# A graph-attention layer on one core: the node stage in two passes, normalization on ScalarE and VectorE, ten early sections gathered raw, and edge targets held in whole sections

## The chip, the cores and the metric

The kernel runs on one core of a Trainium2 chip. The metric is the device time of one execution in microseconds. A core has TensorE (PE, matmuls), VectorE (DVE), ScalarE (ACT), GpSimd (POOL, which here also issues the indirect DMAs that gather rows) and SyncE (SP, which issues most other DMAs).

## The reference

There are N = 12500 nodes with C = 128 channels and E = 400000 edges, sorted by their target node `dst`. Cut to what matters:

```python
h       = relu(layernorm(x))                       # N x 128
msg_src = h @ w_src + b_src                        # N x 128
msg_dst = h @ w_dst                                # N x 128
message = msg_src[src] + msg_dst[dst]              # E x 128
message = message * edge_weight * radial_mlp(edge_attr)
message = message @ w_sep + b_sep                  # E x 256: alpha and value, 8 heads
score   = einsum(smooth_leaky_relu(alpha), alpha_dot)
att     = softmax of score over the edges of one target node
out     = segment_sum(value * att, dst) @ w_proj + b_proj
return x + out
```

## The kernel before, in words

The program has two stages. The **node stage** holds x as 98 tiles of 128 nodes, four to a quad, 25 quads. For a quad, `stats` takes sums by VectorE, `scales` the root (ScalarE) and the reciprocal and shift (VectorE), `norm` the normalized rows (two of four tiles on ScalarE, two on POOL), `turn` four TensorE transposes and one VectorE copy with the relu, and `products(i, k)` the matmuls by w_src (k = 0) or w_dst (k = 1), a ScalarE copy out of PSUM into `ms`, and the store to the tables `t_src` and `t_dst` in HBM, issued by SP. A loop over the quads interleaves these; the w_dst products follow ten quads behind the w_src products.

Between them stand other preparations. `load_targets` brings `dst` on chip as 128 partitions x 3125 targets, and the first and last target of each section and the first of the next by strided DMAs of single words. `falls` compares neighbours for order, `fits` sums the violations into `bad`, `marks` writes a flag for every edge whose target differs from the next (times the constant RESTART) to `same`, `spans`, `cuts` and `direct_ids` prepare windows of target nodes. Everything after the node stage stands behind `if bad == 0`, for which each engine loads `bad` and branches.

The **edge stage** goes over 391 steps k of two sections (f = 0, 1), a section being 512 edges in 4 tiles of 128. For every tile POOL issues one indirect DMA that gathers 128 rows of t_src (line 1018, 8 a step). Steps below 13 (`AHEAD`) have places of their own in `early`, which lie where the messages do (shown as mT in the trace); from step 13 on, the tiles gs0 and gs1 are used with `GSB` = 5 buffers each, so gather k + 5 writes where gather k was read. The first steps, `RAW` = 4 of them, gather rows of x instead of t_src during the node stage (`raw_gather`, 8 a step, line 354). These are normalized and turned (`raw_scales`, `raw_norm`, `raw_turn`) there, and multiplied by w_src in the edge stage (line 1074), where other steps have TensorE transposes of the gathered rows (line 1078). Then line 1095 forms the message `mT` on VectorE, line 1101 multiplies by the alpha weights, and 12 steps later (`LAG`) lines 1233 and 1246 form values and segment sums. `prep_load`, `prep_make` and `prep_turn` bring the source indices of 16 steps, as the gathers need them.

The order of the code is the order on each engine; nothing reorders it. The semaphores say who waits for whom.

Of the kernel before, what the change touches and what calls it, by code (L numbers as in the profile page):

```python
# [44 lines left out]
RAW = 4  # L45
# [10 lines left out]
def gnn_kernel(ctx: ExitStack, tc: tile.TileContext, a: dict, out: bass.AP):  # L56
# [45 lines left out]
    groups = [(t, min(t + XG, NF)) for t in range(0, NF, XG)]  # L102
# [8 lines left out]
    def blocks(t0, t1):  # L111
# [19 lines left out]
    part8 = const.tile([P, 1], F32, name="part8")  # L131
    nc.vector.tensor_scalar(part8, part, float(H), None, op0=ALU.mult)
    spread = const.tile([MQ, P], BF16, name="spread")
    below = const.tile([MQ, P], F32, name="below")
    nc.vector.tensor_scalar(below, lane[:MQ, :], part8[:MQ], None, op0=ALU.subtract)
    above = const.tile([MQ, P], F32, name="above")
    nc.vector.tensor_scalar(above, below, 0.0, None, op0=ALU.is_ge)
    nc.vector.scalar_tensor_tensor(spread, below, float(H), above, op0=ALU.is_lt, op1=ALU.mult)
    spread4 = const.tile([MQ, P], BF16, name="spread4")
    nc.vector.tensor_copy(spread4.rearrange("i (j b h) -> i j b h", j=4, b=4),  # L140
                          spread.rearrange("i (b j h) -> i j b h", b=4, j=4))
# [39 lines left out]
    with tc.tile_pool(name="node", bufs=2) as np_, tc.tile_pool(name="node1", bufs=1) as n1, \  # L181
# [23 lines left out]
        cur = n1.tile([P, CC + 1], I32, name="cur")  # L205
        nc.vector.memset(cur[0:1, 0:1], -1)
        NH = NS // 17
        ends = n1.tile([NH, 17, 2], I32, name="ends")
# [7 lines left out]
        def load_targets():  # L216

            nc.sync.dma_start(out=cur[:, 1:CC + 1], in_=dst.rearrange("(p c) -> p c", p=P))
            at = dst[CC - 1:CC]
            with nc.allow_non_contiguous_dma(reason="single targets"):  # L220
                nc.sync.dma_start(out=cur[1:P, 0:1], in_=bass.AP(at.tensor, at.offset, [[CC, P - 1], [1, 1]]))
                at = dst[0:1]
                h = NH - 1
                nc.sync.dma_start(out=ends[0:h], in_=bass.AP(
                    at.tensor, at.offset, [[34 * SEC // 2, h], [SEC, 17], [SEC - 1, 2]]))
                at = dst[h * 17 * SEC:h * 17 * SEC + 1]
                nc.sync.dma_start(out=ends[h:NH, 0:16, :], in_=bass.AP(
                    at.tensor, at.offset, [[1, 1], [SEC, 16], [SEC - 1, 2]]))
                at = dst[(NS - 1) * SEC:(NS - 1) * SEC + 1]
                nc.sync.dma_start(out=ends[h:NH, 16, :], in_=bass.AP(  # L230
                    at.tensor, at.offset, [[1, 1], [E - 1 - (NS - 1) * SEC, 2]]))
                at = dst[SEC:SEC + 1]
                nc.sync.dma_start(out=nexts[0:h], in_=bass.AP(at.tensor, at.offset, [[17 * SEC, h], [SEC, 17]]))
                at = dst[(h * 17 + 1) * SEC:(h * 17 + 1) * SEC + 1]
                nc.sync.dma_start(out=nexts[h:NH, 0:16], in_=bass.AP(at.tensor, at.offset, [[1, 1], [SEC, 16]]))

        nexts = n1.tile([NH, 17], I32, name="nexts")
        nc.vector.memset(nexts, 0)
# [50 lines left out]

        def scales(t0, t1):  # L290
            s = slice(t0, t1)
            nc.scalar.activation(rstd[:, s], mv[:, s, 2], AF.Sqrt, bias=eps, scale=1.0 / C)
            nc.vector.reciprocal(rstd[:, s], rstd[:, s])
            nc.vector.scalar_tensor_tensor(shift[:, s], mv[:, s, 1], -1.0, rstd[:, s],
                                           op0=ALU.mult, op1=ALU.mult)

        def norm(i):
            t0, t1 = quads[i]
            hs[i] = np_.tile([P, 4, C], F32, name="h", bufs=4)
            for t in range(t0, t1):  # L300
                n = rows(t)
                if t - t0 < 4 - 2:
                    nc.scalar.activation(hs[i][:n, t - t0, :], x_all[:n, t, :], AF.Identity,
                                         bias=shift[:n, t:t + 1], scale=rstd[:n, t:t + 1])
                else:
                    nc.gpsimd.tensor_scalar(hs[i][:n, t - t0, :], x_all[:n, t, :], rstd[:n, t:t + 1],
                                            shift[:n, t:t + 1], op0=ALU.mult, op1=ALU.add)
# [50 lines left out]
        def raw_scales(q0, q1):  # L358
# [6 lines left out]
            nc.scalar.activation(rstdr[:, s], mvr[:, s, 2], AF.Sqrt, bias=eps, scale=1.0 / C)  # L365
            nc.vector.reciprocal(rstdr[:, s], rstdr[:, s])
            nc.vector.scalar_tensor_tensor(shiftr[:, s], mvr[:, s, 1], -1.0, rstdr[:, s],
                                           op0=ALU.mult, op1=ALU.mult)

        def raw_norm(q):  # L370
            v = raw(q).rearrange("p (t c) -> p t c", c=C)
            hs["raw", q] = h = np_.tile([P, 4, C], F32, name="h", bufs=4)
            for t in range(4):
                u = slice(4 * q + t, 4 * q + t + 1)
                if t < 2:
                    nc.scalar.activation(h[:, t, :], v[:, t, :], AF.Identity, bias=shiftr[:, u], scale=rstdr[:, u])
                else:
                    nc.vector.tensor_scalar(h[:, t, :], v[:, t, :], rstdr[:, u], shiftr[:, u],
                                            op0=ALU.mult, op1=ALU.add)
# [17 lines left out]

        gt = n1.tile([P, CC], BF16, name="gt")

# [5 lines left out]
        def fits():  # L405
            cnt = n1.tile([P, 1], F32, name="cnt")
            nc.vector.memset(cnt, 0.0)
            span = n1.tile([NH, 2, 17], F32, name="span")
# [4 lines left out]
            nc.vector.tensor_reduce(cnt[:NH, :], span.rearrange("p a b -> p (a b)"), AX.X, ALU.add)  # L413
            tot = nps.tile([1, BANK], F32, name="tot", bufs=1)
            for o in range(0, CC, BANK):
                w = min(BANK, CC - o)
                nc.tensor.matmul(tot[:, :w], ones_b, gt[:, o:o + w], start=(o == 0), stop=False,
                                 skip_group_check=True)
# [16 lines left out]
            nc.sync.dma_start(out=ends_d[:, 1:2 * NS + 1].rearrange("o (p c) -> (o p) c", p=NH),  # L435
                              in_=ends.rearrange("p s i -> p (s i)"))
# [94 lines left out]
        sm = n1.tile([P, CC], BF16, name="sm")  # L531
        past = n1.tile([1, NX + 1 - E], BF16, name="past")

        def marks(j):
            s_ = slice(j * CC // 4, (j + 1) * CC // 4)
            nc.vector.tensor_tensor(sm[:, s_], cur[:, s_], cur[:, s_.start + 1:s_.stop + 1], op=ALU.not_equal)
            nc.vector.tensor_scalar(sm[:, s_], sm[:, s_], RESTART, None, op0=ALU.mult)
            if j == 3:
                nc.sync.dma_start(out=same[:, 0:E].rearrange("o (p c) -> (o p) c", p=P), in_=sm)
                nc.sync.dma_start(out=same[:, E:NX + 1], in_=past)  # L540

        for i in range(3):
            stats(*quads[i])
            scales(*quads[i])
            norm(i)
            if i == 0:
                turn(0)
                nc.gpsimd.memset(past, RESTART)
                first()
        for i in (3, 4):  # L550
            stats(*quads[i])
        scales(quads[3][0], quads[4][1])
        more = iter(weights_list())
        for i in range(Q):
# [10 lines left out]
            if i % 2 and i + 4 < Q:  # L565
                scales(quads[i + 4][0], quads[min(i + 5, Q - 1)][1])
# [19 lines left out]
            if i == 22:  # L586
                direct_ids()
        for t in range(Q, 4 * RQ):
            raw_gather(t)
        for i in range(Q - 10, Q):  # L590
            q = i - (Q - 10)
            products(i, 1)
            if 0 <= q - 1 < RQ:
                raw_turn(q - 1)
            if q in (1, 4):
                raw_scales(4 + q // 2, 6 + q // 2)
            if q < RQ:
                raw_norm(q)
        nc.scalar.activation(silu, eps[0:1, :], AF.Silu)

# [312 lines left out]
    def windows():  # L913
# [7 lines left out]
        with tc.tile_pool(name="ps", bufs=1, space=PSUM) as pp, \  # L921
# [568 lines left out]
            def step(k):  # L1490
# [20 lines left out]
                if k % 16 == 8 and has(k + 8):  # L1511
# [337 lines left out]
```

## Time and profile before

| what | us |
|---|---|
| runs before (median of 3) | 4083.88 (4075.56 to 4085.45) |
| profiled execution, its own time | 4089.07 |
| its span | 4087.2 |
| mean granted TensorE clock | 0.985 |
| TensorE busy | 3865.2 (95%) |
| VectorE busy | 3104.5 (76%) |
| POOL busy | 3065.6 (75%) |
| ScalarE busy | 1862.3 (46%) |

In rows of the profile a line number (L1018) is one of the kernel before; "out<-in" names what is written and read, "xN" counts instructions; a timeline row begins with the start and the duration in us and ends with the idle time before it and what released it. A group row has the busy sum, the mean of one in ns, and the idle time before its instructions. In a table of windows the columns are the window, its length, and the busy time (with count) of PE, PEld, DVE and POOL for the named tile, the granted clock, the share of DMA time and GB/s.

### The profile page before, as it was taken

The numbers are of one execution on the slowest core, as the hardware profiler recorded it, in microseconds if no ns is written. First come the engines' busy times: TensorE is split into PE (matmuls) and PEld (weight loads), VectorE is DVE, ScalarE is ACT, GpSimd is POOL, SyncE is SP. The second block draws the span as 40 slices with busy tenths as digits, with TensorE's granted clock in tenths as the row PEclk, the third lists the DMA queues.
The fourth block names the chain that finished last, engine by engine and source line by source line (L and its number), as shares of the span: only waits on it lengthen the run. The fifth ranks groups of instructions, "written<-read, shape, count | busy, mean of one in ns | idle before, by whom it ended". The sixth has DMA issues, their size and how long they took to land.

```text
span 4087.2 us, 84249 instructions
## 1 busy us (share of the span) xinstructions
PE 3865.2 (95%) x27811; PEld 2349.3 (57%) x27811; DVE 3104.5 (76%) x5557; ACT 1862.3 (46%) x3782; POOL 3065.6 (75%) x3244
## 2 busy tenths in 40 slices
PE   7899999999999999999999999999999999999997
PEld 6356555655555555555555555555555556556555
DVE  6677777777777777777777777777777777777777
ACT  5454444444444444444444444444444444444451
POOL 6777777777777777777777777777777777777775
PEclk9999999999999999999999999999999999999998
DMA  7777777677767777777777777777777777777772
GB/s 242 214 186 194 182 193 193 184 182 190 191 169 195 186 191 172 196 187 180 185 192 185 190 189 197 194 174 192 197 194 183 185 191 198 182 195 193 186 177 55
DMA packets 536579, 762.21 MB, mean 186 GB/s; under 512 B 126743, under 2 KB 339769, under 8 KB 536006
## 3 DMA queue, kind: packets, MB, share of 16 engines
q1 hardware_dynamic: 378142, 498.27, 41.8%
q0 software_dynamic: 101872, 207.34, 24.5%
q10 hardware_dynamic: 56120, 51.10, 4.5%
q8 instruction: 226, 3.70, 0.4%
q14 instruction: 219, 1.79, 0.2%
HBM read 632.27 MB, written 125.70 MB: 185 GB/s over the span
## 4 chain that ended last, share of the span: by engine, by line
PE 68%; DMA 12%; POOL 7%; issue 5%; DVE 5%; ACT 2%; SPq 1%; ACTq 0%; DVEq 0%; POOLq 0%
PE V L1233 15%; PE pa L1101 14%; DMA gs<-t_src,idx 8%; PE misc L1246 8%; PE pm L1078 7%; PE p L1062 6%; POOL gs L1018 6%; PE m L1034 5%; PE pm L1090 4%; PE p L1047 4%; PE m L1118 3%; DMA agg<-ob 1%; DVE mT L1095 1%; POOL mT L1018 1%; DMA win<-ob 1%
## 5 line engine op out<-in xcount | busy, mean ns | idle before, releaser
L1018 POOL DMA_INDIRECT gs<-t_src,idx x3021 | 2875.4, 952 | 923.0 <-issue 768.5
L1103 ACT ACTIVATE sl<-pa,c_b_a 128x512 f32<-128x512 f32 x782 | 537.6, 687 | 1089.2 <-PE pa L1101 1085.1
L1108 DVE SCALAR_TENSOR_TENSOR al<-pa,sl 128x512 f32<-128x512 f32 x782 | 536.8, 686 | 527.6 <-ACT sl L1103 520.5
L1233 PEld LDWEIGHTS V<-c_w_v,mT 128*128 128x128 f32 x6154 | 753.3, 193 | 309.9 <-DVE ob L1250 119.9
L1233 PE MATMUL V<-c_w_v,mT 128*128 128x128 f32 x6154 | 886.3, 287 | 8.1 <-DVE pvx L1235 8.1
L1101 PE MATMUL pa<-mT,c_w_a 128*128 128x512 f32 x1564 | 839.2, 619 | 26.6 <-DVE mT L1095 23.5
L1235 DVE TENSOR_TENSOR pvx<-V,Pem 128x512 f32<-128x512 f32 x770 | 528.4, 686 | 207.9 <-PE V L1233 191.1
L1049 ACT ACTIVATE h<-p,b 128x512 f32<-128x512 f32 x391 | 469.2, 1200 | 427.5 <-PE p L1047 328.4
L1078 PEld LDWEIGHTS pm<-ident,gs 128*128 128x128 f32 x3021 | 375.2, 141 | 481.9 <-issue 463.8
L1067 DVE SCALAR_TENSOR_TENSOR rad<-p,c_fc_b,w_b 128x1024 f32<-128x1024 f32 x391 | 500.5, 1280 | 105.6 <-PE p L1062 87.3
L1246 PEld LDWEIGHTS misc<-pvx,oh 128*64 128x64 f32 x6250 | 353.1, 138 | 295.0 <-ACT h L1037 284.5
L1078 PE MATMUL pm<-ident,gs 128*128 128x128 f32 x3021 | 458.6, 275 | 64.5 <-DMA gs<-t_src,idx 64.4
L1095 DVE SCALAR_TENSOR_TENSOR mT<-pm,c_b_src,rad 128x1024 f32<-128x1024 f32 x391 | 497.6, 1273 | 7.7 <-PE pm L1090 7.2
L1246 PE MATMUL misc<-pvx,oh 128*64 128x136 f32 x6250 | 453.2, 287 | 0.9 <-ACT h L1037 0.3
L1062 PE MATMUL p<-h,w3b 64*128 64x512 f32 x1564 | 405.9, 596 | 0.5 <-ACT h L1049 0.4
L1034 PE MATMUL m<-eT,w1b 64*128 64x256 f32 x782 | 276.7, 434 | 20.3 <-ACT qT L1328 15.1
L1090 PE MATMUL pm<-ohT,m 64*128 64x512 f32 x1564 | 287.3, 445 | 0.0
L1101 PEld LDWEIGHTS pa<-mT,c_w_a 128*128 128x128 f32 x1564 | 237.3, 192 | 76.8 <-DVE mT L1095 44.5
L1034 PE MATMUL misc<-eT,w1b 64*128 64x256 f32 x782 | 276.8, 434 | 0.0
L1037 ACT ACTIVATE h<-misc,b 128x256 f32<-128x256 f32 x391 | 185.4, 474 | 193.9 <-PE misc L1034 181.1
L1134 ACT ACTIVATE Sp<-m,b_s 128x512 f32<-128x512 f32 x192 | 131.8, 686 | 308.5 <-PE m L1118 302.0
L1217 DVE TENSOR_TENSOR oh<-lane,misc 128x504 f32<-128x504 f32 x391 | 261.2, 668 | 0.1
(216 smaller groups left out, 3550.8 us busy)
## 6 DMA issues: line engine op xcount, KB each, us to landing
w_b<-in_edge_weight SPq DMA_DIRECT2D x390, 512.0 KB
d_b<-in_dst SPq DMA_DIRECT2D x390, 256.0 KB
e_t<-in_edge_attr ACTq DMA_DIRECT2D x386, 128.0 KB
sc_d<-Sp SPq DMA_DIRECT2D x192, 256.0 KB
gs<-t_src,idx POOLq DMA_INDIRECT x3021
win<-ob SPq DMA_DIRECT2D x390, 68.0 KB
agg<-ob SPq DMA_DIRECT2D x762, 33.5 KB
md<-t_dst SPq DMA_DIRECT2D x782, 32.0 KB
```

The source lines that it names most:

```text
L1018: sent = [nc.gpsimd.indirect_dma_start(out=gs[:, t, :], out_offset=None, in_=t_src[:, :], in_offset=bass.IndirectOffsetOnAxis(ap=idx[:, t0 ...
L1034: nc.tensor.matmul(p1[f], w1b[s, :], eTs[k][s, :], start=True, stop=True)
L1062: nc.tensor.matmul(p3[:, f, 0:SEC], w3b[s, :], h2s[k][s, :], start=True, stop=True)
L1067: nc.vector.scalar_tensor_tensor(rad[:, 0:n], p3.rearrange("c f e -> c (f e)")[:, 0:n], b3, w_g[k][:, 0:n], op0=ALU.add, op1=ALU.mult)
L1078: turned = [nc.tensor.matmul(pm[:, t * T:(t + 1) * T], gs[:, t, :], ident, start=(t == 0), stop=False, is_transpose=True, skip_group_check ...
L1095: nc.vector.scalar_tensor_tensor(mTs[k][:, 0:n], pms.rearrange("c f e -> c (f e)")[:, 0:n], b_n, rad[:, 0:n], op0=ALU.add, op1=ALU.mult)
L1101: nc.tensor.matmul(pa[:, 0:n], w_a, mTs[k][:, f * SEC:f * SEC + n], start=True, stop=True)
L1103: nc.scalar.activation(sl[:, 0:n], pa[:, 0:n], AF.Silu, bias=b_a, scale=1.0)
L1108: nc.vector.scalar_tensor_tensor(al, pa, 0.25, sl, op0=ALU.mult, op1=ALU.add)
L1233: nc.tensor.matmul(V[:, t, :], mTs[c][:, o:o + T], w_v, start=True, stop=True)
L1235: nc.vector.tensor_mul(pvx[c][:, f, 0:n, 0:C].rearrange("p t (h k) -> p t h k", h=H), V[:, 0:n, :].rearrange("p t (h k) -> p t h k", h=H), ...
L1246: nc.tensor.matmul(acc[f * W:(f + 1) * W, :], ohs[c][:, f * TS + t, :], pvx[c][:, f, t, :], start=(t == 0), stop=(t == n - 1), skip_group_ ...
```

## The change

The node stage is written as two passes over the quads: the first has all w_src products, the second all w_dst products and, between them, the raw rows' work, the marks and the preparations. The roots are split from the other scales. The normalized rows come from ScalarE (three of four tiles, in every third quad four) and VectorE; POOL has only two tiles of each of the first two quads. `RAW` is 5, so ten sections are gathered as rows of x, all 40 gathers issued at once after the first indices. The targets lie as 112 partitions of 7 whole sections (3584), with the word before and after; first and last targets are copied from them by VectorE (`sections`). `marks` has one operation, without RESTART, which the matrix `spread` now carries. The index preparations of the first steps are issued earlier, and the table load of the silu stands inside the second pass. The first load of x has 4 tiles of each partition.

```diff
-RAW = 4
+RAW = 5
...
-    groups = [(t, min(t + XG, NF)) for t in range(0, NF, XG)]
+    groups = [(max(t, 0), min(t + XG, NF)) for t in range(4 - XG, NF, XG)]
...
-        CC = E // P
+        SPP = -(-NS // P)
+        CC, CP = SPP * SEC, -(-NS // SPP)
+        CL = E - (CP - 1) * CC
+        SL = -(-CL // SEC)
+        assert 96 <= CP - 1 < P and 0 < CL < CC
...
-            nc.sync.dma_start(out=cur[:, 1:CC + 1], in_=dst.rearrange("(p c) -> p c", p=P))
-            at = dst[CC - 1:CC]
+            h = CP - 1
+            nc.sync.dma_start(out=cur[0:h, 1:CC + 1], in_=dst[0:h * CC].rearrange("(p c) -> p c", c=CC))
+            nc.sync.dma_start(out=cur[h:CP, 1:CL + 1], in_=dst[h * CC:E].rearrange("(p c) -> p c", p=1))
             with nc.allow_non_contiguous_dma(reason="single targets"):
-                nc.sync.dma_start(out=cur[1:P, 0:1], in_=bass.AP(at.tensor, at.offset, [[CC, P - 1], [1, 1]]))
-                at = dst[0:1]
-                h = NH - 1
-                nc.sync.dma_start(out=ends[0:h], in_=bass.AP(
-                    at.tensor, at.offset, [[34 * SEC // 2, h], [SEC, 17], [SEC - 1, 2]]))
...
+        def sections():
+
+            for e in range(2):
+                nc.vector.tensor_copy(ends[:, :, e], cur[:, 1 + e * (SEC - 1):1 + e * (SEC - 1) + (SPP - 1) * SEC + 1:SEC])
...
+        def roots(t0, t1):
+            s = slice(t0, t1)
+            nc.scalar.activation(rstd[:, s], mv[:, s, 2], AF.Sqrt, bias=eps, scale=1.0 / C)
+
         def scales(t0, t1):
             s = slice(t0, t1)
-            nc.scalar.activation(rstd[:, s], mv[:, s, 2], AF.Sqrt, bias=eps, scale=1.0 / C)
...
-                if t - t0 < 4 - 2:
+                if t - t0 < (2 if i < 2 else 4 if i % 3 == 0 else 3):
...
-                    nc.gpsimd.tensor_scalar(hs[i][:n, t - t0, :], x_all[:n, t, :], rstd[:n, t:t + 1],
+                    (nc.gpsimd if i < 2 else nc.vector).tensor_scalar(hs[i][:n, t - t0, :], x_all[:n, t, :], rstd[:n, t:t + 1],
...
-                if t < 2:
+                if t < 3:
...
             nc.vector.tensor_tensor(sm[:, s_], cur[:, s_], cur[:, s_.start + 1:s_.stop + 1], op=ALU.not_equal)
-            nc.vector.tensor_scalar(sm[:, s_], sm[:, s_], RESTART, None, op0=ALU.mult)
...
+        nc.vector.memset(past, 1.0)
+        for i in range(2):
             stats(*quads[i])
+            roots(*quads[i])
             scales(*quads[i])
             norm(i)
-            if i == 0:
-                turn(0)
-                nc.gpsimd.memset(past, RESTART)
-                first()
-        for i in (3, 4):
+        turn(0)
+        first()
+        for t in range(4 * RQ):
+            raw_gather(t)
+        for i in range(2, 5):
             stats(*quads[i])
-        scales(quads[3][0], quads[4][1])
+            if i == 2:
+                roots(*quads[i])
+                scales(*quads[i])
+                norm(i)
+        ready = quads[3][0], quads[4][1]
+        roots(*ready)
         more = iter(weights_list())
         for i in range(Q):
             if i + 1 < Q:
                 turn(i + 1)
+            if ready:
+                scales(*ready)
+                ready = None
             if i + 3 < Q:
                 norm(i + 3)
-            raw_gather(i)
-            if i >= 10:
-                products(i - 10, 1)
             products(i, 0)
             if i + 5 < Q:
                 stats(*quads[i + 5])
             if i % 2 and i + 4 < Q:
-                scales(quads[i + 4][0], quads[min(i + 5, Q - 1)][1])
+                ready = quads[i + 4][0], quads[min(i + 5, Q - 1)][1]
+                roots(*ready)
...
-            if 8 <= i < 12:
-                falls(i - 8)
-            if i == 13:
+            if i == 9:
+                sections()
+            if 10 <= i < 14:
+                falls(i - 10)
+            if i == 15:
                 fits()
-            if 14 <= i < 18:
-                marks(i - 14)
-            if i >= 9 and i % 4 == 1:
-                raw_scales(i // 4 - 2, i // 4 - 1)
-            if i == 19:
-                spans()
-            if i == 21:
-                cuts()
-            if i == 22:
-                direct_ids()
-        for t in range(Q, 4 * RQ):
-            raw_gather(t)
-        for i in range(Q - 10, Q):
-            q = i - (Q - 10)
+        extra = {2: lambda: marks(0), 4: lambda: marks(1), 6: lambda: marks(2), 8: lambda: marks(3),
+                 10: spans, 13: cuts, 15: direct_ids, 17: spreads}
+        assert 2 * RQ + 1 < Q
+        for i in range(Q):
+            if i % 2 and 0 <= i // 2 - 1 < RQ:
+                raw_turn(i // 2 - 1)
             products(i, 1)
-            if 0 <= q - 1 < RQ:
-                raw_turn(q - 1)
-            if q in (1, 4):
-                raw_scales(4 + q // 2, 6 + q // 2)
-            if q < RQ:
-                raw_norm(q)
-        nc.scalar.activation(silu, eps[0:1, :], AF.Silu)
-
+            if i % 4 == 0 and i // 2 < RQ:
+                raw_roots(i // 2, i // 2 + 2)
+            if i % 4 == 1 and i // 2 < RQ:
+                raw_scales(i // 2, i // 2 + 2)
+            if i % 2 and i // 2 < RQ:
+                raw_norm(i // 2)
+            if i in extra:
+                extra[i]()
+            if i == 2 * RQ - 2:
+                nc.scalar.activation(silu, eps[0:1, :], AF.Silu)
...
-                if k % 16 == 4 and has(k + 12):
+                if k % 16 == 4 and has(k + 12) and k > 4:
                     prep_load((k + 12) // 16)
-                if k == 2:
-                    prep_load(0)
+                if k in (-1, 0):
+                    prep_load(k + 1)
...
-                    prep_turn((k + 8) // 16)
-                if k == 4:
-                    prep_make(0)
-                if k % 16 == 7 and has(k + 9):
+                if k == 5 or k % 16 == 8 and has(k + 8) and k > 8:
+                    prep_turn((k + 11) // 16)
+                if k in (2, 4):
+                    prep_make(k // 2 - 1)
```

The order of instructions on POOL in the node stage, around the first raw gather, before (the names: h are normalized rows, mT the places of raw rows and early gathers, idx the source indices):

```order
19 L306 TENSOR_SCALAR h<-x_all,rstd,shift 128x128 [waits DMAHW4_49,DVE_49]
20 L306 TENSOR_SCALAR h<-x_all,rstd,shift 128x128
21 L354 DMA mT<-in_x,idx_172 128x128
22 L306 TENSOR_SCALAR h<-x_all,rstd,shift 128x128 [waits PE_49,Activation_49]
23 L306 TENSOR_SCALAR h<-x_all,rstd,shift 128x128
24 L354 DMA mT<-in_x,idx_172 128x128
25 L306 TENSOR_SCALAR h<-x_all,rstd,shift 128x128 [waits DVE_49,PE_49,Activation_49]
```

and of the change:

```order
12 L299 TENSOR_SCALAR h<-x_all,rstd,shift 128x128 [waits DMAHW1_49,DVE_49]
13 L299 TENSOR_SCALAR h<-x_all,rstd,shift 128x128
14 L299 TENSOR_SCALAR h<-x_all,rstd,shift 128x128 [waits DMAHW4_49,DVE_49]
15 L299 TENSOR_SCALAR h<-x_all,rstd,shift 128x128
16 L347 DMA mT<-in_x,idx_164 128x128 [waits DVE_49]
17 L347 DMA mT<-in_x,idx_164 128x128 x7
```

The pairs of normalizations between the raw gathers (they go on in the same way up to row 80) are gone, and the gathers stand together, ahead of the load of `bad`.

On TensorE, in the middle of the node stage before (pt are transposes, pm products):

```order
114 L315 MATMUL pt<-ident,h 128x128 [waits PE_49,Activation_49]
115 L315 MATMUL pt<-ident,h 128x128 [waits Activation_49]
116 L315 MATMUL pt<-ident,h 128x128 [waits Pool_49] x2
117 L326 MATMUL pm<-w_dst,x_all 128x128 [waits Activation_49]
118 L326 MATMUL pm<-w_dst,x_all 128x128 x3
119 L326 MATMUL pm<-w_src,x_all 128x128 [waits DVE_49,Activation_49]
120 L326 MATMUL pm<-w_src,x_all 128x128 x3
```

and of the change, at the border between the passes:

```order
138 L319 MATMUL pm<-w_src,x_all 128x128 [waits DVE_49]
139 L319 MATMUL pm<-w_src,x_all 84x128 [waits DMAHW3_49]
140 L319 MATMUL pm<-w_dst,x_all 128x128 [waits Activation_49]
141 L319 MATMUL pm<-w_dst,x_all 128x128 x3
142 L319 MATMUL pm<-w_dst,x_all 128x128 [waits Activation_49]
143 L319 MATMUL pm<-w_dst,x_all 128x128 x3
144 L319 MATMUL pm<-w_dst,x_all 128x128 [waits Activation_49]
145 L319 MATMUL pm<-w_dst,x_all 128x128 x3
146 L381 MATMUL pt<-ident,h 128x128 [waits Activation_49] x3
147 L381 MATMUL pt<-ident,h 128x128 [waits DVE_49]
```

The w_dst products no longer stand between the w_src products; they follow all of them, with the raw rows' transposes (line 381) among them.

More of the change, by code (lines that the diff above doesn't have):

```diff
@@ L201, in gnn_kernel @@
         b12 = const.tile([P, 2], F32, name="b12")
[L202 removed]
+        SPP = -(-NS // P)
[3 more added lines that the diff above has]
+        assert 96 <= CP - 1 < P and 0 < CL < CC
         ones_b = n1.tile([P, 1], BF16, name="ones_b")
         nc.vector.memset(ones_b, 1.0)
[L205 removed]
+        cur = n1.tile([CP, CC + 2], I32, name="cur")
         nc.vector.memset(cur[0:1, 0:1], -1)
[L207 to L208 removed]
+        nc.vector.memset(cur[96:CP, CL + 1:CC + 2], 0)
+        ends = n1.tile([CP, SPP, 2], I32, name="ends")
         eb = n1.tile([P, NS, 2], I32, name="eb")
@@ L396, in first @@
             nc.vector.tensor_copy(idx0, pt)
-        gt = n1.tile([P, CC], BF16, name="gt")
+        gt = n1.tile([CP, CC], BF16, name="gt")
         def falls(j):
@@ L407, in fits @@
             nc.vector.memset(cnt, 0.0)
-            span = n1.tile([NH, 2, 17], F32, name="span")
+            span = n1.tile([CP, 2, SPP], F32, name="span")
+            nexts = cur[:, 1 + SEC:2 + CC:SEC]
             nc.vector.tensor_sub(span[:, 0, :], ends[:, :, 1], ends[:, :, 0])
@@ L412, in fits @@
             nc.vector.tensor_scalar(span[:, 1, :], span[:, 1, :], float(W), None, op0=ALU.is_ge)
-            nc.vector.tensor_reduce(cnt[:NH, :], span.rearrange("p a b -> p (a b)"), AX.X, ALU.add)
+            nc.vector.tensor_reduce(cnt[:CP, :], span.rearrange("p a b -> p (a b)"), AX.X, ALU.add)
             tot = nps.tile([1, BANK], F32, name="tot", bufs=1)
[L415 to L418, printed above, removed]
+            assert CL >= BANK
+            for n, o0, o1 in ((CP, 0, CL), (CP - 1, CL, CC)):
+                for o in range(o0, o1, BANK):
+                    w = min(BANK, o1 - o)
+                    nc.tensor.matmul(tot[:, :w], ones_b[:n], gt[:n, o:o + w], start=(o == 0), stop=False,
+                                     skip_group_check=True)
             nc.tensor.matmul(tot[:, 0:1], cnt, ones[:, 0:1], start=False, stop=True, skip_group_check=True)
```

56 lines of the change are left out of this document (28 added, 28 removed).

## The prediction

> **What bounds the kernel now.** I read the page first, for the chain that ended last and the costliest groups.
>
> ```profile
> span 4087.2 us, 84249 instructions
> ...
> PE 3865.2 (95%) x27811; PEld 2349.3 (57%) x27811; DVE 3104.5 (76%) x5557; ACT 1862.3 (46%) x3782; POOL 3065.6 (75%) x3244
> ...
> PE 68%; DMA 12%; POOL 7%; issue 5%; DVE 5%; ACT 2%; SPq 1%; ACTq 0%; DVEq 0%; POOLq 0%
> ...
> L1018 POOL DMA_INDIRECT gs<-t_src,idx x3021 | 2875.4, 952 | 923.0 <-issue 768.5
> ```
>
> TensorE looks like the bound, 95% busy. But matmuls that are held count as busy here, and POOL's 75% hides that its gathers never pause: each is 0.95 us busy and the idle time ahead of them is almost all "issue", time in which POOL waits for nothing. So I asked for the same tile in equal windows far apart.
>
> ```profile
> 500.00:1000.00 500.00, 61.84 (x408) 50.76 (x408) 0.00 (x0) 377.76 (x398) 1.00 0.72 185
> 3000.00:3500.00 500.00, 59.13 (x392) 48.56 (x393) 0.00 (x0) 378.81 (x398) 0.99 0.74 192
> ```
>
> The last count of four is POOL's: 398 gathers in 500 us in both, 1.256 us each, 8 a step, 10.05 us a step. Then the two ends of this queue, from the timeline, with the last two stores of t_src.
>
> ```profile
> 89.92 0.32 SPq L340 DMA_DIRECT2D t_src<-ms  x1
> 90.33 0.39 SPq L342 DMA_DIRECT2D t_src<-ms  x1
> ...
> 93.89 0.94 POOL L1018 DMA_INDIRECT mT<-t_src,idx  x1 [2.97 <-DMA t_src<-ms]
> ...
> 3981.30 0.94 POOL L1018 DMA_INDIRECT gs<-t_src,idx  x1 [0.30 <-PE m L1334]
> ```
>
> Between them stand 3093 gathers (3125 tiles of 128 edges less the 32 raw ones): 3981.30 - 93.89 = 3887.4, over 3092 intervals 1.257 us each, the same as in any window, so the queue has no hole. So the time is: when the first table gather starts (it waits for the last store of t_src), plus the gathers, plus a tail of about 105 us. The change touches the first two.
>
> What limits how early the queue may run is its buffers: gather k+5 writes where the transposes of step k read. The tightest place is the first reuse, step 13 second section, against gather 18; beside it stands step 17 against gather 22.
>
> ```profile
> 227.76 0.60 PE L1078 MATMUL pm<-ident,gs 128*128 128x128 f32 x4
> 239.07 0.94 POOL L1018 DMA_INDIRECT gs<-t_src,idx  x1 [0.30 <-issue]
> ...
> 264.86 0.60 PE L1078 MATMUL pm<-ident,gs 128*128 128x128 f32 x4
> ...
> 279.06 0.95 POOL L1018 DMA_INDIRECT gs<-t_src,idx  x1 [0.30 <-issue]
> ```
>
> Read at 228.36, overwritten from 239.07: 10.7 us to spare; four steps later 265.46 and 279.06, 13.6. So the queue can move earlier by 10.7 us against TensorE's first 13 steps, not by more; after that TensorE, faster than 10.05 us a step here, gives way by itself.
>
> **The change, part by part.** The node stage's prices come from the groups of its first 112 us (busy sum, mean of one).
>
> ```profile
> L354 POOL DMA_INDIRECT mT<-in_x,idx x32 | 32.0, 1001 | 6.7 <-issue 6.0 <-PE pt L315 0.3 <-DVE ids_d L516 0.3
> L326 PE MATMUL pm<-w_src,x_all 128*128 128x128 f32 x196 | 31.0, 308 | 7.9 <-DVE x_all L317 7.4 <-ACT h L303 0.4
> L326 PE MATMUL pm<-w_dst,x_all 128*128 128x128 f32 x196 | 29.7, 302 | 0.0
> L332 ACT COPY ms<-pm 128x512 f32<-128x512 f32 (+2 forms) x52 | 27.9, 554 | 20.9 <-PE pm L326 18.7 <-issue 1.9
> L303 ACT ACTIVATE h<-x_all,shift,rstd 128x128 f32<-128x128 f32 (+1 forms) x50 | 21.9, 486 | 5.9 <-DVE shift L294 5.9
> L315 PE MATMUL pt<-ident,h 128*128 128x128 f32 x98 | 20.5, 315 | 13.6 <-POOL h L306 9.5 <-ACT h L303 3.4
> L317 DVE TENSOR_SCALAR x_all<-pt 128x512 f32<-128x512 f32 (+1 forms) x25 | 16.6, 666 | 3.0 <-PE pt L315 3.0
> L385 PE MATMUL pt<-ident,h 128*128 128x128 f32 x32 | 7.0, 310 | 4.6 <-ACT h L376 4.2 <-DVE h L378 0.2
> L292 ACT ACTIVATE rstd<-mv,eps 128x8 f32<-128x8 f32 (+2 forms) x14 | 4.2, 304 | 9.8 <-DVE mv L287 9.7
> L536 DVE TENSOR_TENSOR sm<-cur 128x781 bf16<-128x781 int32 (+1 forms) x4 | 3.9, 963 | 0.0
> ```
>
> *Pass 1 (t_src).* ScalarE becomes its longest engine: 79 normalizations instead of 50, at 21.9/50 = 0.438 us, are 34.6; 25 copies at 27.9/52 = 0.537 are 13.4; 14 roots at 0.30 are 4.2; together 52.2. TensorE has 20.5 + 31.0 = 51.5 with less ahead of it, so ScalarE sets the end. It starts and first waits as the next rows show, since this beginning is nearly the same.
>
> ```profile
> L303 ACT ACTIVATE h<-x_all,shift,rstd x50: 477/484/498, 7.2 to 77.1; 128x128 f32<-128x128 f32 x49, 84x128 f32<-84x128 f32 x1
> ...
> 11.55 0.30 ACT L292 ACTIVATE rstd<-mv,eps 128x4 f32<-128x4 f32 x1 [3.46 <-DVE mv L287]
> ...
> 20.05 7.03 SPq L224 DMA_DIRECT2D ends<-in_dst  x1
> ...
> 36.60 0.59 ACT L332 COPY ms<-pm 128x512 f32<-128x512 f32 x1 [5.60 <-PE pm L326]
> ```
>
> 7.2 + 3.5 + 52.2 = 62.9, and 11 waits for the scales, 5.9 us before (the L303 row); the split of root and scales puts VectorE's turn copy (0.67, L317) between, so up to 0.54 + 0.67 = 1.2 each: 5.9 to 13.2. The last copy ends at 69 to 76; I take 71.5, since the order lets a copy fill most of these waits. The 7.03 us in which SP issued single words, with the 5.60 us stall of copies behind it, goes: that is why I add no such stall. From the last store's issue to the first gather took 93.89 - 90.33 = 3.6, and about 0.4 more lie between copy and issue: first table gather at 75.5, 18.4 earlier.
>
> *Raw gathers.* 40 at 1.00 + 0.30 issue from about 11 us on are 52, over at 63: hidden by pass 1 with 12 us over; if the ids come late by more, they delay the queue one for one. Eight table gathers fewer are 8 x 1.257 = 10.1. The queue by itself would so end 28.5 us earlier.
>
> *Pass 2 (t_dst, raw rows, marks).* It begins on TensorE near 70.5. TensorE: w_dst 29.7 and 40 raw transposes at 7.0/32 = 0.219, 8.8: 38.5. ScalarE: 26 copies 14.0, 30 raw normalizations 13.1, 5 roots 1.5, the table load 1.5: 30. VectorE about 30 (raw rows' statistics, norms and turns, four marks at 0.963 x 896/781 = 1.10, spans, cuts). So TensorE bounds it. Late in the stage it ran faster:
>
> ```profile
> 107.80 0.94 PE L326 MATMUL pm<-w_dst,x_all 128*128 128x128 f32 x7
> ...
> 109.66 0.69 DVE L386 TENSOR_SCALAR mT<-pt 128x512 f32<-128x512 f32 x1 [0.50 <-PE pt L385]
> 110.02 0.42 ACT L332 COPY ms<-pm 128x128 f32<-128x128 f32 x2 [0.66 <-PE pm L326]
> ```
>
> 0.94 for 7 is 1.07 a quad of eight, 26.9 for 25 quads instead of 29.7: 35.7 to 38.5. With 0.8 for the last copies and 0 to 4 of gaps, pass 2 ends at 107 to 113.8. I take 110.5; before, it ended at 110.44. So the stage as a whole ends where it did: the work is the same, only its order differs.
>
> *One more raw step.* The step's start in VectorE's mT rows (steps 0, 3, 4 and 7):
>
> ```profile
> 123.78 1.28 DVE L1095 SCALAR_TENSOR_TENSOR mT<-pm,c_b_src,rad 128x1024 f32<-128x1024 f32 x1
> 150.09 1.28 DVE L1095 SCALAR_TENSOR_TENSOR mT<-pm,c_b_src,rad 128x1024 f32<-128x1024 f32 x1
> 156.91 1.27 DVE L1095 SCALAR_TENSOR_TENSOR mT<-pm,c_b_src,rad 128x1024 f32<-128x1024 f32 x1
> 179.62 1.27 DVE L1095 SCALAR_TENSOR_TENSOR mT<-pm,c_b_src,rad 128x1024 f32<-128x1024 f32 x1
> ```
>
> Three raw steps took 26.31/3 = 8.8 us each, three others 22.71/3 = 7.6: step 4 becomes 1.2 longer. The moved loads and makes of the gather indices (steps -1, 0, 2, 4, 5) add nothing to the first 13 steps, only change their order; on SP six small DMAs now stand ahead of later md loads, at 0.4 us each, which I leave at nothing to +2.
>
> *The sum.* Step 13 is read 0.1 + 1.2 us later, rounded 1.2 (bounds -3 to +7), so gather 18 comes 10.7 - 1.2 = 9.5 us earlier (3.7 to 13.7), and from there all that follows. About 19 of the 28.5 us turn into POOL waiting for TensorE at gathers 18 and after. Marks without the second operation, and targets without single words, save time off the path beyond the stall named: nothing. The profiled execution, 4089.07 with a span of 4087.2, would come to 4079.6. It lies 5.2 above the median of the runs, 4083.88; from that median, 4074.4.
>
> **A rule against a row.** One gather was caught beneath a VectorE operation with two inputs from SBUF:
>
> ```profile
> 42.89 0.95 DVE L403 TENSOR_TENSOR gt<-cur 128x781 bf16<-128x781 int32 x1
> 42.92 1.77 POOL L354 DMA_INDIRECT mT<-in_x,idx  x1 [0.16 <-issue]
> ```
>
> 1.77 instead of 1.00 on average: 0.77 longer. Four marks, the spans and a few target compares now stand beneath table gathers: 4 to 7 of them, 3 to 5 us on the queue. They lie ahead of gather 18, where POOL has 19 us to spare, so I count nothing; if that wait isn't there, they come off the gain.
>
> The Trainium skill ("SBUF — State Buffer", section "Who interferes with whom") has tensor_tensor contend with GpSimd's reads alone, and not hold up the making of DMA descriptors, so by it this term would be nothing in either case. The row above disagrees.
>
> **Rivals.**
> *A, the early start counts in full.* Queue alone: 4083.9 - 28.5 = 4055.4. It needs step 13 read at least 18 us earlier. For it: if pass 2 ran at the transposes' later pace (four in 0.60 above, 0.15 each against 0.219), TensorE would need 38.5 x 0.69 = 26.4 and ScalarE's 30 would bound: end at about 102, step 13 some 7.7 earlier, gain 18.4, 4065.5. Against: products wait for nothing between in the w_dst row (idle 0.0) and still took 29.7. Chance 0.27 for 4055 to 4070.
> *B, pass 2 stretches.* Gathers now run through it, some 27 or more, each 0.94 us; if VectorE is held through them, its 30 us become 55 to 67, pass 2 ends at 127 to 139, step 13 is read 18 to 30 us later. From 10.7 on, the queue is later than before: 4083.9 + 7.3 to 19.3, 4091 to 4103. For it: the 1.77 row (there POOL paid). Against: the turn copy at 109.66 took 0.69 between gathers, 0.67 on average before them. Chance 0.15.
> *C, only the eight gathers count.* If the raw ids or pass 1 come late so that the first table gather stays near 93.9: 10.1 less, 4073.8, as long as step 13 allows it. Chance 0.06.
> My own case has the remaining 0.52, 4070 to 4080.
>
> **Numbers.** A change within 0.3% (12.3 us) can't be told from none here. Faster by more: A and a quarter of my case, 0.27 + 0.13 = 0.40. Slower by more: B and what lies beyond, 0.18. Within: 0.42. The range leaves out the lower fifth of A and B's half: 4058 to 4091; my case alone 4070 to 4080.
>
> **What would show it.** First table gather near 75; last t_dst copy near 110 and step 0's mT near 124; POOL sitting idle for PE just ahead of gathers 18 and 19, some 19 us in all; then 398 gathers per 500 us again; last gather near 3972. Wrong if POOL never waits there (A), if step 13 is read past 239 (B), or if the spacing of later gathers changes.

## The result, and the profile after

The change is slower: 4094.22 us (median of 11 runs) against 4084.17 before, ratio 1.0024 with a 95% interval of 1.0013 to 1.0036. The profiled execution took 4092.9 us. In one later session (second block of experiments) the chip took 5244 us for the kernel before as well, with all engines idle in stretches where the profile names no cause, so its times are not used, nor is one execution of 6281.32 us in the session after it.

The page first, then the table of the gathers' windows. The lines are those of before plus 18 here: 1036 gathers, 1096 transposes, 1113 mT.

```profile
span 4091.1 us, 84238 instructions
...
PE 3864.8 (94%) x27816; PEld 2340.9 (57%) x27816; DVE 3107.1 (76%) x5569; ACT 1880.1 (46%) x3824; POOL 3036.2 (74%) x3199
...
L1036 POOL DMA_INDIRECT gs<-t_src,idx x3021 | 2871.7, 951 | 942.1 <-issue 764.8
```

```profile
500.00:1000.00 500.00, 62.40 (x416) 52.27 (x416) 0.00 (x0) 378.39 (x400) 1.00 0.71 186
3000.00:3500.00 500.00, 60.15 (x396) 48.42 (x396) 0.00 (x0) 378.68 (x399) 1.00 0.72 191
```

The steady part is the same queue, 399 or 400 gathers in 500 us against 398. So the loss is made before it. The places that the prediction named, from the timeline:

```profile
95.37 0.94 POOL L1036 DMA_INDIRECT mT<-t_src,idx  x1 [32.39 <-DVE shiftr L363]
...
143.30 1.28 DVE L1113 SCALAR_TENSOR_TENSOR mT<-pm,c_b_src,rad 128x1024 f32<-128x1024 f32 x1
173.17 1.28 DVE L1113 SCALAR_TENSOR_TENSOR mT<-pm,c_b_src,rad 128x1024 f32<-128x1024 f32 x1
...
246.39 0.94 POOL L1036 DMA_INDIRECT gs<-t_src,idx  x1 [20.56 <-PE pm L1096]
...
251.47 0.60 PE L1096 MATMUL pm<-ident,gs 128*128 128x128 f32 x4
...
252.34 0.94 POOL L1036 DMA_INDIRECT gs<-t_src,idx  x1 [1.27 <-PE pm L1096]
```

The first table gather comes at 95.37, not near 75. The mT of step 0 comes at 143.30, not near 124. Step 13's second section is read until 252.07, 23.7 us later than before. And POOL waits 20.56 us at gather 18, for exactly the transposes that the prediction named. That this is near the 19 us that it gave is chance, since the first table gather and step 13 both came some 20 us late. Gather 18's second section starts at 252.34, 13.3 us later than the 239.07 of before: 23.7 less the 10.7 that there were to spare.

Not all of the 13.3 us reaches the end in this one execution. The last gather starts at 3988.46, 7.2 us after the 3981.30 of before (the prediction had it near 3972), because the gathers behind gather 18 run 1.2554 us apart on average, and 1.2575 before. Why is not shown; in a run below with the same code but for the queue of one load it was 1.2567, so single executions differ by much of this.

Where the 20 us of the node stage went, from the timeline of SP, ScalarE and VectorE:

```profile
19.98 0.28 SPq L214 DMA_DIRECT2D cur<-in_dst  x1
...
22.37 23.03 SPq L241 DMA_DIRECT2D lim<-in_dst  x1
```

```profile
51.78 0.59 ACT L325 COPY ms<-pm 128x512 f32<-128x512 f32 x1 [17.13 <-DMA t_src<-ms]
...
48.66 0.25 DVE L226 COPY ends<-cur 112x7 int32<-112x7 int32 x2 [13.05 <-DMA lim<-in_dst]
```

SP issues the load of the targets (line 214, 111 partitions) in 0.28 us, and then stands for 23.03 us in the issue of a load of four words. The stores of t_src are queued behind it on SP, ScalarE's copies wait 17.13 us for `ms` buffers that these stores would free, and VectorE waits 13.05 us at its first copy out of the targets (the row names a load of the limits, but the copy reads `cur`, whose last rows land at 47.8 us by the trace's packets). The same 20 us in a table of windows (PE, PEld, DVE, ACT and POOL busy, granted clock, share of DMA time, GB/s), of the change:

```profile
24.00:44.00 20.00, 10.47 (x68) 7.66 (x66) 9.37 (x27) 9.05 (x24) 15.11 (x17) 0.87 0.35 120
```

The 16 DMA engines are busy 35% of the time, though SP, ScalarE and VectorE stand waiting for DMAs in much of it. The packets of the load of the targets have 14336 bytes; 93 of them lie in 24 to 44 us, and by their durations 2.6 were in flight at a time, beside POOL's gathers. The whole load runs from 21.5 to 47.3 us.

The Trainium skill ("DMA: Bandwidth & Descriptors", section "Why a DMA increments its semaphore by 16 and not by 1") says that a DMA of this kind runs on the largest number of engines up to 16 that divides its slowest dimension, and names 16 for 96 or 128 partitions; by this rule, as an estimate, 111 partitions get 3. The 2.6 packets in flight agree, and so do the next two runs.

### The profile page after: what moved, and what is told of

It is laid out like the page before. It is cut to its first block, busy times and chain, and to the rows that moved or that the text cites. A ratio compares the mean times of both kernels' runs of the same rounds, so it can differ in the third digit from the quotient of the medians.

```text
span 4091.1 us, 84238 instructions
## 1 busy us (share of the span) xinstructions
PE 3864.8 (94%) x27816; PEld 2340.9 (57%) x27816; DVE 3107.1 (76%) x5569; ACT 1880.1 (46%) x3824; POOL 3036.2 (74%) x3199
## 4 chain that ended last, share of the span: by engine, by line
PE 62%; DMA 13%; POOL 10%; issue 7%; DVE 4%; ACT 2%; SPq 1%; ACTq 0%; DVEq 0%; POOLq 0%
PE V L1251 13%; PE pa L1119 12%; DMA gs<-t_src,idx 9%; POOL gs L1036 9%; PE misc L1264 7%; PE p L1080 6%; PE pm L1096 6%; PE m L1052 4%; PE pm L1108 4%; PE p L1065 3%; PE m L1136 3%; DVE mT L1113 1%; DMA agg<-ob 1%; DMA cur<-in_dst 1%; POOL mT L1036 0%
## 5 line engine op out<-in xcount | busy, mean ns | idle before, releaser
L1119 PEld LDWEIGHTS pa<-mT,c_w_a 128*128 128x128 f32 x1564 | 236.6, 191 | 75.5 <-DVE mT L1113 42.5
L1065 PE MATMUL p<-h,w2b 64*64 64x256 f32 x3128 | 260.5, 403 | 2.7 <-DVE rad L1085 2.7
```

The lines of the kernel that those rows point to most:

```text
L1119: nc.tensor.matmul(pa[:, 0:n], w_a, mTs[k][:, f * SEC:f * SEC + n], start=True, stop=True)
```

## The experiments: the load of 111 partitions

**The load cut in two.** The change, and nothing else but this:

```diff
-            nc.sync.dma_start(out=cur[0:h, 1:CC + 1], in_=dst[0:h * CC].rearrange("(p c) -> p c", c=CC))
+            for p0, p1 in ((0, 96), (96, h)):
+                nc.sync.dma_start(out=cur[p0:p1, 1:CC + 1],
+                                  in_=dst[p0 * CC:p1 * CC].rearrange("(p c) -> p c", c=CC))
```

> The change with the load of the targets cut into 96 and 15 partitions, nothing else. In the change SP's next DMA issue after that load was held 23.0 us (22.37 to 45.45), ScalarE's copies stood 17.1 us for ms buffers and VectorE 13.1 us for the targets; in that stretch only 2.6 packets of the load were in flight at a time. Theory (the 111-partition load runs on three DMA engines, and that hold is the whole delay): the hold falls to a few us, the first table gather comes at 74 to 80, step 0's mT near 125, step 13's second section is read near 234, POOL waits for it at gather 18, and the time is 4 to 6 us below before, about 4079. Rival (pass 1 is slow for its own waits between roots, scales and copies, the hold covers them): first gather still beyond 85, 4087 or more. Rival B of the prediction (gathers stretch pass 2): first gather near 76, but step 0's mT beyond 135, 4090 or more.

Measured: 4083.68 us, ratio to before 0.9998 (0.9989 to 1.0007), so 10 us less than the change. The window of above, SP's loads of the limits, the first table gather and the wait at gather 18 (lines two higher):

```profile
24.00:44.00 20.00, 15.03 (x92) 10.63 (x93) 13.83 (x40) 15.76 (x40) 14.15 (x15) 1.00 0.86 201
...
L243 SPq DMA_DIRECT2D lim<-in_dst x4: 603/746/3954, 22.7 to 32.1; - x4
...
81.54 0.94 POOL L1038 DMA_INDIRECT mT<-t_src,idx  x1 [17.82 <-DMA t_dst<-ms]
...
129.60 1.28 DVE L1115 SCALAR_TENSOR_TENSOR mT<-pm,c_b_src,rad 128x1024 f32<-128x1024 f32 x1
...
229.77 0.94 POOL L1038 DMA_INDIRECT gs<-t_src,idx  x1 [17.83 <-PE pm L1098]
...
235.72 0.95 POOL L1038 DMA_INDIRECT gs<-t_src,idx  x1 [1.26 <-PE pm L1098]
```

DMA share 0.86 instead of 0.35, the longest issue 3.95 us instead of 23.03, the first table gather 13.8 us earlier, step 0's mT 13.7. By its packets the load now runs from 22.2 to 32.3 us, with nearly 16 packets in flight at its peak. That is the theory's side, and the change's loss is gone. The theory's own times were missed, though: the first table gather lies outside 74 to 80, step 0's mT is 4.6 us behind 125, gather 18 comes only 3.4 us ahead of before (235.72 against 239.07), and instead of the expected 4 to 6 us no gain over before can be told.

**The same cost put into the kernel before.** Its load of 128 partitions is cut into 111 and 17:

```diff
-            nc.sync.dma_start(out=cur[:, 1:CC + 1], in_=dst.rearrange("(p c) -> p c", p=P))
+            for p0, p1 in ((0, 111), (111, P)):
+                nc.sync.dma_start(out=cur[p0:p1, 1:CC + 1],
+                                  in_=dst[p0 * CC:p1 * CC].rearrange("(p c) -> p c", c=CC))
```

> The kernel before with its load of the targets cut into 111 and 17 partitions, the same bytes to the same places. Theory: the load takes some 20 us or more on three engines (37 rows of 0.5 us each), SP is held behind it, t_src is stored later, and since the queue of before has no slack the whole delay reaches the end: first table gather 105 to 115 instead of 93.9, time 4096 to 4106. Rival (a split load costs nothing, the change's delay has another cause): first gather at 94 and 4084.

Measured: 4108.32, ratio 1.0055 (1.0040 to 1.0070).

```profile
L226 SPq DMA_DIRECT2D ends<-in_dst x1: 29177/29177/29177, 20.7 to 20.7; - x1
...
ACT ms L334 <- DMA t_src<-ms: 27.7, 1, 27.7
...
117.07 0.94 POOL L1020 DMA_INDIRECT mT<-t_src,idx  x1 [3.74 <-DMA t_src<-ms]
```

SP's issue of the sections' ends, which is held behind this load, takes 29.2 us instead of 7.03, and the first table gather comes at 117.07 instead of 93.89, 23.2 us later. The median is 22.9 us above that session's before (4085.47): without slack in the queue, the delay passes through whole, a little beyond what was expected. The trace shows why it is beyond: the load's 128 rows run from 20.9 to 49.6 us, some 2.8 in flight at a time up to 40 us, and from 41.6 on one at a time, 0.47 us each. These are 17 rows, as many as the second piece has, and they take 8 us: 17 partitions divide worse still than 111. So the cost of a load's cut by partition count is shown, with nothing else of the change, but the 23 us belong to both pieces and not to the 111 partitions alone.

**Another queue for it.** In the change, the 111-partition load goes out from ScalarE's queue (`nc.scalar.dma_start`), uncut.

> The change with the 111-partition load issued by ScalarE's queue instead of SP's, uncut. SP isn't held by it then, but the targets land as late. If SP's hold alone is the delay, it is like the run with the cut load: first table gather 74 to 80, about 4079. If the late landing counts as well (VectorE stands at the copies of the first and last targets, in the middle of pass 1), first gather 85 to 92 and 4086 to 4092. If neither, as the change, 4094.

Measured: 4096.98, ratio 1.0027 (1.0016 to 1.0037), the third answer.

```profile
L241 SPq DMA_DIRECT2D lim<-in_dst x4: 604/746/15054, 21.9 to 51.1; - x4
...
100.39 0.94 POOL L1036 DMA_INDIRECT mT<-t_src,idx  x1 [37.40 <-DVE shiftr L363]
```

SP isn't relieved: its four small loads of the limits still start between 21.9 and 51.1. So the expectation's premise, that SP's queue is free when another engine issues the load, failed. The trace shows two holds. The first small load stands 15.05 us in its issue, to 37.0. The second starts only at 49.55, 0.8 us after the last packet of the big load (48.8); these DMAs use eight semaphores (counters of completion) in turn, and it is the first to reuse that of the big load, so here SP waits for that load itself. The first hold is of another kind, since that small load has a different semaphore, and so are the 23.03 us in the change, which end at 45.40, 1.9 us ahead of the big load's last packet. How the issue is held there (by the loads of single words behind the big one on the same DMA engines, for instance) these runs don't settle.

## The experiments: what the early start is worth

**Four raw steps instead of five**, with the cut load (`RAW = 4`):

> The change with the cut load and four raw steps instead of five: eight table gathers more (10.1 us of queue), one raw step less. Theory (gather 18 waits for TensorE's step 13, so the length of the queue before it has slack): no longer than with five, by the raw step 0 to 2 us shorter, 4076 to 4080, POOL's wait at gather 18 some 10 us shorter. Rival (the queue is the bound from its first gather on): 10 us longer than with five.

Measured: 4077.69, ratio 0.9981 (0.9972 to 0.9990), against 0.9998 with five.

```profile
226.95 0.94 POOL L1038 DMA_INDIRECT gs<-t_src,idx  x1 [5.31 <-PE pm L1098]
```

Eight gathers more, 10.1 us of queue, and the kernel is 6 us faster: they fill POOL's wait, which is 5.31 instead of 17.83, and gather 18's second section comes 2.8 us earlier (232.90). Of these, 2.6 lie ahead of step 0 (its mT at 127.0 instead of 129.6), where single executions differ by as much (last section), so what the raw step itself costs is not shown. The direction is the theory's; the size is above the 0 to 2 us that were expected, and gather 18 accounts for only half of it.

**Six buffers for gathered sections.** The place comes from two other tiles:

```diff
-GSB = 5
+GSB = 6
...
-                al = sp.tile([C, SEC], F32, name="al", bufs=6)[:, 0:tiles(k, f) * T]
+                al = sp.tile([C, SEC], F32, name="al", bufs=5)[:, 0:tiles(k, f) * T]
...
-                nodes[g] = sp.tile([P, P + 2], I32, name="node", bufs=2)
+                nodes[g] = sp.tile([P, P + 2], I32, name="node", bufs=1)
```

Five and four raw steps with it, their control and one further edit ran first with a kernel before at 5244 us. Their ratios there were 1.0059, 1.0048, 1.0034 and 1.0024; none of the expected times can be judged by them.

> The change with the cut load, five raw steps and six buffers for gathered sections instead of five; the place comes from the alpha tile (five buffers instead of six) and a small tile of node numbers (one instead of two). Theory (gather 18 waits for step 13 to be read): now gather 19 waits for it, one step of 10.05 us later in the queue, so all gathers from there are about 10 us earlier than with five buffers: last gather near 3964, time 8 to 11 us less than the same with five buffers (4083.7), 4073 to 4076. Rival (the end is set by TensorE or by something else than the queue): within 3 us of 4083.7.

> The same with four raw steps. There POOL stood only about 5 us ahead of gather 18, so theory: this wait goes and nothing takes its place, POOL's gathers run without a hole from the first, 3093 x 1.257 after about 81 us, last gather near 3968; 4 to 6 us less than with five buffers (4077.7), 4072 to 4074. Rival as above: within 2 us of 4077.7.

> The change with the cut load, four raw steps, five gather buffers, but the alpha tile and the node numbers cut as in the two runs before: what those cuts cost by themselves. If nothing, 4076 to 4080; if later waits for alpha buffers matter, 4082 or more, and the two runs before hide a gain of that size.

> The change with the cut load, four raw steps, and the loads of single words (111 partitions) cut into 96 and 15 as well. In the run with the cut load alone SP was still held 10.0 us at the next loads. If these words on three engines are what holds it, the hold falls under 5 us, the first table gather comes 2 to 5 us earlier (76 to 79); since gather 18 waits for step 13, the time follows only as far as pass 2 ends earlier too: 4073 to 4078. If the big load itself is the hold, SP still stands about 10 us and nothing changes: 4076 to 4079.

Of the last one, the first 36 us lie ahead of the idle stretches and can be read:

```profile
L245 SPq DMA_DIRECT2D lim<-in_dst x4: 604/738/748, 24.4 to 34.2; - x4
```

The limits' loads are issued from 24.4 to 34.2, no sooner than with uncut words (22.7 to 32.1): the words are not the hold that is left. Part of what is left is again a wait for the big load: in both runs its packets go on to 32.3 us, and SP stands 6.7 us (3.9 with uncut words) ahead of the small load that reuses its semaphore and starts at 31.82 (32.13). What this edit does to the time is unknown. The other three were repeated in a session with before at 4083.77.

> The change with the cut load, five raw steps and six buffers, once more, against a kernel before near 4085. Theory (gather 18 waits for step 13): now gather 19 waits for it, about 10 us earlier in the queue than with five buffers (second section of gather 19 near 236 instead of 245.7), last gather near 3964, ratio to before near 0.997. Rival (TensorE or something else sets the end): ratio as with five buffers, 0.9998.

> The same with four raw steps. Theory: no wait at gather 18 or 19 is left, the queue runs without a hole from about 81 us; second section of gather 19 near 237, last gather near 3968, ratio near 0.997, within 2 us of the run with five raw steps. Rival: ratio as with five buffers, 0.998.

> The change with the cut load, four raw steps and five gather buffers, with the alpha tile and the node numbers cut as in the two runs before: the cuts' own cost. If nothing, ratio 0.998; if waits for alpha buffers matter, 1.000 or more, and the two runs before hide a gain of that size.

| cut load, and | ratio to before | interval |
|---|---|---|
| five raw steps, five buffers | 0.9998 | 0.9989 to 1.0007 |
| five raw steps, six buffers | 0.9977 | 0.9967 to 0.9988 |
| four raw steps, five buffers | 0.9981 | 0.9972 to 0.9990 |
| four raw steps, five buffers, small tiles cut | 0.9986 | 0.9975 to 0.9996 |
| four raw steps, six buffers | 0.9974 | 0.9963 to 0.9985 |

The first and third rows stand against a before of 4085.47, the others against 4083.77.

The timeline with five raw steps and six buffers at gathers 18 and 19:

```profile
213.68 0.94 POOL L1038 DMA_INDIRECT gs<-t_src,idx  x1 [0.30 <-issue]
...
233.13 0.94 POOL L1038 DMA_INDIRECT gs<-t_src,idx  x1 [9.77 <-PE pm L1098]
```

and with four:

```profile
81.02 0.94 POOL L1038 DMA_INDIRECT mT<-t_src,idx  x1 [28.78 <-DMA t_dst<-ms]
...
222.15 0.94 POOL L1038 DMA_INDIRECT gs<-t_src,idx  x1 [0.30 <-issue]
...
232.15 0.94 POOL L1038 DMA_INDIRECT gs<-t_src,idx  x1 [0.30 <-issue]
```

With five raw steps the wait moves from gather 18 to gather 19, as expected, and the time falls by some 9 us. In this execution gather 19's second section came at 239.08, not near 236 (245.71 with five buffers), since step 13 itself was 3.3 us later than in the run with five. With four, no wait is left at either. There the sixth buffer was worth little: 0.9981 and 0.9986 against 0.9974, within each other's intervals, so theory and rival aren't told apart. The control shows no cost of the cut tiles. The version with four raw steps and six buffers (4071.0 us) is ahead of both kernels.

**Six buffers in the kernel before** (place from the same two tiles and the output tile):

> The kernel before with six gather buffers (place from the alpha tile, node numbers and the output tile, one buffer less each). In before no gather waits for a buffer: theory 4084, ratio 1.000 within 0.002, the same first gather near 94 and the same last one. Rival (more buffers by themselves let the queue or TensorE run better later): ratio below 0.998.

Measured: 4080.56, ratio 1.0000 (0.9988 to 1.0012).

```profile
93.31 0.94 POOL L1018 DMA_INDIRECT mT<-t_src,idx  x1 [3.84 <-DMA t_dst<-ms]
...
234.26 0.94 POOL L1018 DMA_INDIRECT gs<-t_src,idx  x1 [0.30 <-issue]
```

Where no gather waits for a buffer, a buffer more is worth nothing.

## Why the prediction was wrong

*The frame held.* The queue of gathers paces the kernel at nearly the same rate before and after. Its early start is given back at gather 18, which waits for step 13. The rule "step 13 later by d moves the queue by d - 10.7" gave 13.0 us for the measured 23.7, and 13.3 were seen; the run with five raw steps and six buffers moved the wait to gather 19, and before with six buffers gained nothing.

*The step that failed* is the sentence in pass 1 that SP's hold of 7.03 us, with ScalarE's stall of 5.60, goes when the single words go: "that is why I add no such stall". The reading behind it was wrong: the 7.03 us were not the price of single words. By the packets of before, the load of the targets ran to 26.85 us and the hold ended at 27.08; and where that load alone was cut into 111 and 17, with the same single words behind it, the hold grew to 29.18 us and again ended with the load (49.86 against 49.56). So the hold came from the load of the targets, and the change keeps this load. It moves nearly the same bytes in another shape, and I gave that shape no price. It holds SP 23.03 us and ScalarE 17.13 in the change. That is the whole of the loss against before: cutting this load alone took the time from 4094 back to 4084.

*Terms mis-sized beside it.* With the load cut, the first table gather came at 81.54, not 75.5. The last copy of pass 1 (the second of the three in its row) ended at 73.3, not 71.5. Between copy and issue of the last store lay 3.0 us, not 0.4, because the five stores before it went out in a row from 72.86; and from that issue to the gather it took 5.2 us, not 3.6:

```profile
72.86 3.35 SPq L335 DMA_DIRECT2D t_src<-ms  x5
72.92 0.91 ACT L327 COPY ms<-pm 128x128 f32<-128x128 f32 x3 [1.28 <-PE pm L321]
...
76.30 0.59 SPq L337 DMA_DIRECT2D t_src<-ms  x1
...
114.12 0.91 ACT L327 COPY ms<-pm 128x512 f32<-128x512 f32 x3 [0.26 <-PE pm L321]
```

Pass 2 ended at 115.0, 4.5 us later than I took and past the upper bound of 113.8; which of its parts I had too short stays open. So even with the cut load the gain was 3.4 us at gather 18, below the lower bound of 3.7 and not 9.5. Step 13 was then read at 235.45, 7.1 us later than before: 4.6 by the end of pass 2, 1.2 between there and step 0's mT, and 1.3 from there to step 13, close to the 1.2 that I gave the fifth raw step. The steps with the index loads moved ahead took longer in the change, 29.87 us from step 0's mT to step 3's against 26.31 before, but 26.94 with the cut load, so the nothing to 2 that I gave SP's loads there is not refuted.

*The raw step's trade was right in sign.* The eight table gathers that the fifth raw step saves are worth nothing while gather 18 waits, as the sum had it; the run with four raw steps was faster.

*Rivals.* B named the outcome (step 13 18 to 30 us later, 4091 to 4103) by another mechanism, gathers holding VectorE in pass 2. That one did not show: with the cut load, gathers run through the whole of pass 2, and it ends 4.6 us later than before (115.0 against 110.4), not 17 to 29. A fell with the waits at gather 18. C's condition came about, with the first table gather at 95.37 and so near 93.9, but not its time, because step 13 did not allow it: the wait at gather 18 decided, not the eight gathers. The 0.77 us that a gather loses beneath a VectorE operation with two inputs was weighed for 4 to 7 gathers; the last section shows how few it meets.

## What to carry to other kernels

A load is priced by its shape, not by its bytes: ask how the partition count divides among DMA engines (111 here ran about three rows at a time and 17 one, 96 and 15 together up to 16), and what is queued behind it on the queue that issued it. An earlier start of a queue is worth only what its buffers allow: find the first reuse of a buffer, measure the time to spare there, and what reads it last; work moved ahead of that reader then counts one for one. A prefetch that shortens such a queue (the raw rows) pays only while the queue is the bound; here, with its consumer the bound, the kernel with one raw step less was 6 us faster.

## What the runs showed that was not expected

A gather beneath a two-input VectorE operation is stretched only if it begins beneath it. From the timeline of the change:

```profile
56.00 1.07 DVE L399 TENSOR_TENSOR gt<-cur 112x896 bf16<-112x896 int32 x1
56.01 1.88 POOL L347 DMA_INDIRECT mT<-in_x,idx  x1 [0.30 <-issue]
...
95.37 0.94 POOL L1036 DMA_INDIRECT mT<-t_src,idx  x1 [32.39 <-DVE shiftr L363]
95.56 1.08 DVE L537 TENSOR_TENSOR sm<-cur 112x896 bf16<-112x896 int32 x1
```

The gather that started 0.01 us after the VectorE operation took 1.88 us; the one under way for 0.19 us when such an operation started took its usual 0.94. In the ten traces other than those of the 5244 us session, all 39 gathers under way when such an operation on the targets started took 0.94 to 0.98 us, and the seven that began within 0.3 us behind its start took 1.62 to 1.88. The node stage also differs from execution to execution: with the same instructions up to there, the mT of step 0 came at 127.0, 125.8 and 122.5 us in the three profiled executions with four raw steps, so a single profile places step 13 to some 4.5 us only, as much as the terms that the prediction argued over.
